# Two 5x5 convolution layers on one core: rows stored by place in the tile, and GpSimd's differences held behind VectorE's transform

## The chip, the core and the metric

The kernel runs on one core of a Trainium2 chip. The core has five engines that this kernel uses side by side, each with its own queue of instructions worked off in order: TensorE (PE, matrix products), VectorE (DVE) and GpSimd (POOL), which both do elementwise arithmetic, ScalarE (ACT, copies and activations) and SyncE (SP), which here only starts DMA transfers. Data lies in SBUF (128 partitions), matrix products land in PSUM. The metric is the time of one execution on the device, in microseconds; lower is better.

## What is computed

The input is 8 images of 32 channels, 252 x 252, in float32. Two layers are applied one after the other, each `x + conv5x5(group_norm(x))` with reflecting borders:

```python
x = x + _L0_conv_ref(_gn(x), L0_conv_weight)
x = x + _L1_conv_ref(_gn(x), L1_conv_weight)
```

`_gn` normalizes each image over 16 groups of two channels (mean and variance over two channels and all pixels). `_conv_ref` is written with FFTs in the reference, and is a 5 x 5 convolution from 32 to 32 channels.

## The kernel before

**Layout.** Rows and columns of an image are split by parity. The 128 partitions hold 4 quarters of 32 channels, one for each pair (column parity, row parity), so that a 5 x 5 filter becomes a 3 x 3 one on 126 x 126 points with 128 channels in and out. Along the rows the 3-tap filter is done as a minimal-filtering transform (Winograd's F(6,3)): a tile of 8 rows in gives 6 rows out by way of 8 products; along the columns the 3 taps are 3 accumulating matmuls.

**Steps.** An image is cut into 7 steps of 18 output rows (`GR`), each 3 tiles (`NT`) of 6 rows (`TR`). 8 images by 2 layers by 7 make 112 steps. They run in 16 phases of 7: layer 0 of one image alternates with layer 1 of the image before it. The first layer's output goes to a scratch image in DRAM, from which the second layer reads; the second layer's output goes to the result.

**What one step does.**

- `prepare` (lines 135 to 145) brings 20 rows of input into `g`: by ScalarE copies from a fetched `x` for layer 0, by one DMA from the scratch image for layer 1. In `g` row r lies at place r, so tile t's rows 0 to 5 stand together, and each row's 128 columns are contiguous.
- `differences` (336 to 346) on GpSimd: `a` (line 344) and, later, `e` (346), each one operation over 4 rows of all 3 tiles, 128 x 1536 elements, both operands in SBUF.
- `transform` (348 to 370) on VectorE: `e` again, two `v` from `e` (360, 361), `p` from `a` and two `v` from `p`, `q` from `a` and two `v` from `q`. All their operands lie in SBUF. The stt operations appear in the profile as line 358.
- `ends` (372 to 375) on GpSimd: the first and last `v` (called `v07`) from `e`.
- `conv` (378 to 435): 8 products, each of 3 matmuls (which the profile records as 6), into 8 PSUM buffers (`m`). VectorE combines them: `s1`, `d1`, sums and differences of `m3` with `m4` and `m5` with `m6` (these read one PSUM operand and one that ScalarE copied to SBUF as `a1`, `a3`, `a5`), 6 operations that write `yo[0]` to `yo[5]`, 6 that add to them, and two for `m0` and `m7`: 20 operations. `yo[j]` is row j of all three tiles; the stt ones appear as line 403.
- `to_scratch` or `to_output` sends `y` away, `output_sums` and `input_sums` gather the statistics on ScalarE.

**Order.** The kernel writes the order of each engine's queue out by hand. In step i (the loop over `steps`) VectorE does `transform` of step i + 1 and then `conv` of step i; GpSimd does `a` of step i + 2, `ends` of step i + 1, `e` of step i + 2. `a` and `e` have one buffer each, so GpSimd's next `a` waits until VectorE has read the old one, which is at `q`. In the last step of a phase VectorE also computes the next phase's normalization (`variance`, `scales`, lines 288 to 312, on 128 x 1 tiles) and adds the identity to the matrices (`add_own`, 321 to 324), and ScalarE scales the matrices (`scale_matrices`, 319). All DMAs are started from SyncE's queue, in order. They take eight semaphores in turn, and each DMA waits for the one eight before it.

Statistics of an image's input come in 8 chunks (`input_chunk`, `input_sums`), one per step from step s0 - 10 of the phase that starts at step s0, each loaded one step ahead into one of 3 buffers.

## Time and profile before

| | |
|---|---|
| time, median of 3 runs | 2537.83 us (2537.74 to 2537.83) |
| time of the profiled execution | 2537.77 us |
| its span in the profile | 2536.0 us |
| busy: PE, DVE, ACT, POOL | 1946.3, 2402.5, 1303.9, 1081.4 us |
| granted clock of TensorE, mean | 0.885 of full speed |
| DMA | 371.63 MB, mean 147 GB/s |

How to read the profile's lines. A group of instructions is "line engine operation out<-in, partitions x elements, xcount | busy us, mean ns of one | idle time of the engine before them, and what ended it". A line of the timeline is "start us, duration us, engine, line, operation, out<-in, xcount", and several equal instructions in a row are merged into one line, whose duration then reaches from the first start to the last end. A line of the waits is "who <- for whom: us in total, times, longest". A line of the windows is "from:to, length, busy us and count of PE, PEld (weight loads), DVE, ACT and POOL, the clock granted to TensorE, mean busy share of the DMA engines, GB/s". A line of the DMA issues is "out<-in, queue, xcount, KB each, median us from issue to landing". The names leave buffer numbers out: `v` is any of the v tiles.

### The profile page before, as it was taken

How to read it: one execution, taken by the hardware profiler on the slowest of the kernel's cores; microseconds unless marked ns; L12 is line 12 of the kernel's file. 1: busy time of each engine (PE TensorE's matmuls, PEld its weight loads, DVE VectorE, ACT ScalarE, POOL GpSimd, SP SyncE). 2: the span in 40 equal slices, each digit the busy share in tenths (PEclk: the TensorE clock that was granted, in tenths of full speed). 3: DMA queues.
4: the chain of work that ended last, by engine and by line, in shares of the span. 5: the costliest groups of instructions: out<-in, count | busy, mean ns of one | idle time of the engine just before them, and what ended most of it. 6: DMA issues, size and time to landing. Idle time of an engine off the chain costs nothing.

```text
span 2536.0 us, 18838 instructions
## 1 busy us (share of the span) xinstructions
PE 1946.3 (77%) x5440; PEld 1096.3 (43%) x5440; DVE 2402.5 (95%) x3473; ACT 1303.9 (51%) x1537; POOL 1081.4 (43%) x410
## 2 busy tenths in 40 slices
PE   2787868887698786888868687786877878787786
PEld 1344434444354443544434344443544444444443
DVE  6799999999999999999999999999999999999997
ACT  5885436565355644656445564455635655243233
POOL 4744444434344443443444444344444434434441
PEclk9898888889798897988979898897988889889898
DMA  7884546755466554756546476465665645344433
GB/s 224 209 207 102 131 141 197 178 102 136 155 197 141 118 171 122 201 117 131 174 153 168 103 153 192 122 172 114 129 190 168 158 108 124 106 122 143 113 97 74
DMA packets 177272, 371.63 MB, mean 147 GB/s; under 512 B 12944, under 2 KB 152464, under 8 KB 160656
## 3 DMA queue, kind: packets, MB, share of 16 engines
q1 hardware_dynamic: 177168, 370.43, 56.3%
q8 instruction: 43, 0.70, 0.1%
q14 instruction: 61, 0.50, 0.1%
HBM read 235.09 MB, written 135.28 MB: 146 GB/s over the span
## 4 chain that ended last, share of the span: by engine, by line
DVE 66%; PE 13%; issue 8%; DMA 6%; ACT 5%; SPq 1%; DVEq 0%; ACTq 0%
DVE y L403 19%; DVE v L358 16%; PE m L390 13%; DVE e L358 5%; DVE p L358 3%; DVE q L358 3%; DMA scratch<-y 3%; DVE d L411 2%; DVE mr L310 2%; DVE y L432 2%; DVE s L410 2%; DVE v L360 2%; DVE m L427 2%; DMA sx<-in_x_dram 2%; DVE v L361 2%
## 5 line engine op out<-in xcount | busy, mean ns | idle before, releaser
L390 PE MATMUL m<-v,u 128*128 128x378 f32 x5376 | 1935.0, 521 | 406.7 <-DVE d L411 288.7
L390 PEld LDWEIGHTS m<-v,u 128*128 128x128 f32 x5376 | 1082.1, 205 | 1243.5 <-DVE d L411 328.5
L344 POOL TENSOR_TENSOR a<-g 128x1536 f32<-128x1536 f32 x111 | 418.7, 3772 | 1392.4 <-DVE q L358 1303.0
L358 DVE SCALAR_TENSOR_TENSOR v<-q 128x384 f32<-128x384 f32 x224 | 469.3, 2136 | 3.9
L403 DVE SCALAR_TENSOR_TENSOR y<-m,y 128x378 f32<-128x378 f32 x672 | 370.5, 551 | 23.1
L346 POOL TENSOR_TENSOR e<-g 128x1536 f32<-128x1536 f32 x111 | 382.7, 3448 | 8.6
L468 ACT COPY o<-y 64x1134 f32<-64x1134 f32 x224 | 278.0, 1241 | 175.6 <-DVE y L434 159.3
L144 ACT COPY g<-x 64x2520 f32<-64x2520 f32 x112 | 280.4, 2503 | 14.0 <-DMA x<-in_x_dram 12.0
L414 ACT COPY a<-m 128x378 f32<-128x378 f32 x112 | 53.2, 475 | 365.7 <-PE m L390 365.1
L375 POOL TENSOR_TENSOR v<-e 128x768 f32<-128x768 f32 x111 | 236.4, 2130 | 7.7 <-DVE e L358 7.7
L275 ACT ACTIVATE junk<-y 128x2268 bf16<-128x2268 f32 x112 | 234.7, 2095 | 1.4
L358 DVE SCALAR_TENSOR_TENSOR e<-g,e 128x1536 f32<-128x1536 f32 x112 | 195.9, 1749 | 9.6 <-POOL e L346 9.6
L403 DVE SCALAR_TENSOR_TENSOR y<-m,s 128x378 f32<-128x378 f32 x336 | 185.3, 551 | 12.0
L403 DVE SCALAR_TENSOR_TENSOR y<-m,d 128x378 f32<-128x378 f32 x336 | 185.3, 551 | 11.6
L319 ACT ACTIVATE u<-u,mr 128x3072 f32<-128x3072 f32 x15 | 42.8, 2855 | 168.5 <-DVE mr L310 168.5
L269 ACT ACTIVATE sx<-sx 128x2016 f32<-128x2016 f32 x64 | 118.8, 1857 | 19.4 <-DVE sums L266 17.1
L406 ACT ACTIVATE a<-m,off 128x378 f32<-128x378 f32 x112 | 63.8, 570 | 109.6 <-PE m L390 109.4
L358 DVE SCALAR_TENSOR_TENSOR v<-p 128x384 f32<-128x384 f32 x224 | 115.2, 555 | 3.9
L296 ACT ACTIVATE std<-var 128x1 f32<-128x1 f32 x16 | 3.2, 203 | 220.9 <-DVE var L294 220.9
L358 DVE SCALAR_TENSOR_TENSOR p<-a 128x768 f32<-128x768 f32 x112 | 107.0, 955 | 0.0
L358 DVE SCALAR_TENSOR_TENSOR q<-a 128x768 f32<-128x768 f32 x112 | 106.4, 950 | 0.0
L268 ACT ACTIVATE sx<-sx 128x2016 f32<-128x2016 f32 (+1 forms) x56 | 103.6, 1850 | 3.8 <-DMA sx<-in_x_dram 3.2
(68 smaller groups left out, 1017.6 us busy)
## 6 DMA issues: line engine op xcount, KB each, us to landing
g<-scratch SPq DMA_DIRECT2D x56, 1280.0 KB, 9.7
scratch<-y SPq DMA_DIRECT2D x224, 288.0 KB, 3.9
out_dram<-o SPq DMA_DIRECT2D x224, 283.5 KB, 4.0
sx<-in_x_dram SPq DMA_DIRECT2D x56, 1008.0 KB, 7.8
x<-in_x_dram SPq DMA_DIRECT2D x88, 630.0 KB, 8.7
u<-raw SPq DMA_DIRECT2D x15, 1536.0 KB, 10.5
x<-in_x_dram SPq DMA_DIRECT2D x16, 598.5 KB, 7.0
sx<-in_x_dram SPq DMA_DIRECT2D x8, 882.0 KB, 9.8
```

The lines of the kernel that those rows point to most:

```text
L144: nc.scalar.copy(g[halves[pc], :, 1 - pc : 1 - pc + NB], t[:, :, 1 - pc : W : 2])
L268: nc.scalar.activation(t, t, AF.Identity, accum_out=st[:, 0, c : c + 1])
L269: nc.scalar.activation(t, t, AF.Square, accum_out=st[:, 1, c : c + 1])
L275: nc.scalar.activation(junk, view, (AF.Identity, AF.Square)[k], accum_out=st[:, k, T : T + 1])
L344: v.tensor_sub(rows(a), rows(high[:, :, 1:5]), rows(low[:, :, 1:5]))
L346: return lambda: v.tensor_add(rows(e), rows(high[:, :, 2:6]), rows(low[:, :, 0:4]))
L358: stt = lambda o, i0, c, i1: v.scalar_tensor_tensor(o, i0, c, i1, ALU.mult, ALU.add)
L375: v.tensor_sub(rows(vt[b, l, T].pop()), rows(e[:, :, 2:4]), rows(e[:, :, 0:2]))
L390: nc.tensor.matmul(ps, u[:, f, b3, :], vs[f][:, :, 2 - b3 : 2 - b3 + NB], start=(b3 == 0), stop=(b3 == 2),)
L403: stt = lambda o, i0, c, i1: v.scalar_tensor_tensor(o, i0, c, i1, ALU.mult, ALU.add)
L406: nc.scalar.activation(a1, m1, AF.Identity, bias=offset[b, l])
L468: nc.scalar.copy(o[halves[s], :, 1 - pc : W : 2], yr[halves[pc], s * half : (s + 1) * half, 1 : 1 + NB])
```

## The change

Rows are reordered everywhere from (tile, place in the tile) to (place in the tile, tile): in `g` (which now holds 8 places by 3 tiles, so that the two rows shared by neighbouring tiles are stored twice), `a`, `e`, `p`, `q`, `v07`, `y` and the scratch image. A slice by place, such as `yo[j]` or `a[:, 0:2]`, is now one contiguous range. In `transform` the operations are reordered, in `conv` the order of the places. `g` is filled by four ScalarE copies instead of two, or by three DMAs instead of one; the scratch image takes four DMAs per column parity and step instead of two, the result twelve per step instead of four. The input statistics' chunks come two per step, from step s0 - 7 on. And GpSimd's `a` gets an added dependency on the last operation of the last `transform`.

```diff
 GR = TR * NT
 IR = GR + 2
+DR = TR + 2
...
-        g = gpool.tile([P, IR, PB], F32, tag="g", name=f"g_{b}_{l}_{T}")
+        g = gpool.tile([P, DR, NT, PB], F32, tag="g", name=f"g_{b}_{l}_{T}")
         gt[b, l, T] = g
         if l:
-            nc.sync.dma_start(g, scratch[b][:, GR * T : GR * T + IR, :])
+            nc.sync.dma_start(g[:, 0:TR], scratch[b][:, T])
+            nc.sync.dma_start(g[:, TR:DR, 0 : NT - 1], scratch[b][:, T, 0:2, 1:NT])
+            nc.sync.dma_start(g[:, TR:DR, NT - 1], scratch[b][:, T + 1, 0:2, 0])
             return
...
-            nc.scalar.copy(g[halves[pc], :, 1 - pc : 1 - pc + NB], t[:, :, 1 - pc : W : 2])
-        pad_columns(g.rearrange("p r k -> p (r k)"), 0)
+            cols = slice(1 - pc, W, 2)
+            to = g[halves[pc], :, :, 1 - pc : 1 - pc + NB]
+            nc.scalar.copy(to[:, 0:TR], t[:, 0:GR, cols].rearrange("p (t j) w -> p j t w", j=TR))
+            nc.scalar.copy(to[:, TR:DR], t[:, 2:IR, cols].rearrange("p (t j) w -> p j t w", j=TR)[:, TR - 2 : TR])
+        pad_columns(g.rearrange("p j t k -> p (j t k)"), 0)
...
-        a = apool.tile([P, NT, 4, PB], F32, tag="a", name=f"a_{n}")
-        e = apool.tile([P, NT, 4, PB], F32, tag="e", name=f"e_{n}")
-        v.tensor_sub(rows(a), rows(high[:, :, 1:5]), rows(low[:, :, 1:5]))
+        a = apool.tile([P, 4, NT, PB], F32, tag="a", name=f"a_{n}")
+        e = apool.tile([P, 4, NT, PB], F32, tag="e", name=f"e_{n}")
+        ins = v.tensor_sub(rows(a), rows(g[:, 3:7]), rows(g[:, 1:5]))
         at[b, l, T] = a, e
-        return lambda: v.tensor_add(rows(e), rows(high[:, :, 2:6]), rows(low[:, :, 0:4]))
+        return ins, lambda: v.tensor_add(rows(e), rows(g[:, 4:8]), rows(g[:, 0:4]))
...
-        stt(rows(e), rows(low[:, :, 2:6]), -17 / 4, rows(e))
-        v.tensor_add(vs[0], e[:, :, 2], e[:, :, 1])
-        v.tensor_sub(vs[1], e[:, :, 2], e[:, :, 1])
+        stt(rows(e), rows(g[:, 2:6]), -17 / 4, rows(e))
+        stt(rows(p), rows(a[:, 0:2]), -1 / 4, rows(a[:, 2:4]))
+        v.tensor_add(vs[0], e[:, 2], e[:, 1])
+        v.tensor_sub(vs[1], e[:, 2], e[:, 1])
         yield
-        stt(rows(p), rows(a[:, :, 0:2]), -1 / 4, rows(a[:, :, 2:4]))
-        stt(vs[2], p[:, :, 0], 2.0, p[:, :, 1])
-        stt(vs[3], p[:, :, 0], -2.0, p[:, :, 1])
-        stt(rows(q), rows(a[:, :, 0:2]), -4.0, rows(a[:, :, 2:4]))
-        stt(vs[4], q[:, :, 0], 0.5, q[:, :, 1])
-        stt(vs[5], q[:, :, 0], -0.5, q[:, :, 1])
+        stt(rows(q), rows(a[:, 0:2]), -4.0, rows(a[:, 2:4]))
+        stt(vs[2], p[:, 0], 2.0, p[:, 1])
+        stt(vs[3], p[:, 0], -2.0, p[:, 1])
+        stt(vs[4], q[:, 0], 0.5, q[:, 1])
+        last["transform"] = stt(vs[5], q[:, 0], -0.5, q[:, 1])
...
-        yr = y[:, 0 : GR * PB].rearrange("p (t r k) -> p t r k", r=TR, k=PB)
-        yo = [yr[:, :, j, 1 : 1 + NB] for j in range(TR)]
+        yr = y[:, 0 : GR * PB].rearrange("p (j t k) -> p j t k", j=TR, k=PB)
+        yo = [yr[:, j, :, 1 : 1 + NB] for j in range(TR)]
...
-        for j, c in enumerate((1.0, 2.0, 4.0, 8.0, 16.0, 32.0)):
-            stt(yo[j], m3 if j % 2 else m4, c, d1 if j % 2 else s1)
+        for j in (1, 0, 3, 2, 5, 4):
+            stt(yo[j], m3 if j % 2 else m4, 2.0**j, d1 if j % 2 else s1)
...
-        for j, c in enumerate((1.0, 1 / 2, 1 / 4, 1 / 8, 1 / 16, 1 / 32)):
-            stt(yo[j], m5 if j % 2 else m6, c, yo[j])
+        for j in (5, 0, 1, 2, 3, 4):
+            stt(yo[j], m5 if j % 2 else m6, 0.5**j, yo[j])
...
-            scratch[b] = dram.tile([P, PB, PB], F32, tag="scratch", name=f"scratch_{b}")
+            scratch[b] = dram.tile([P, NG + 1, TR, NT, PB], F32, tag="scratch", name=f"scratch_{b}")
...
-                put(0, GR, J)
...
+            put(1, (T,), slice(None), slice(None))
+            put(0, (T, slice(1, TR)), slice(0, TR - 1), slice(None))
+            put(0, (T, 0, slice(1, NT)), TR - 1, slice(0, NT - 1))
+            put(0, (T + 1, 0, 0), TR - 1, NT - 1)
...
-            nc.sync.dma_start(dst[1 - pr, :, first : first + half, :], o[quads[2 * s + pr]])
+            for t in range(NT):
+                nc.sync.dma_start(dst[1 - pr, :, t, js, :], o[quads[2 * s + pr], t])
...
-                at_step = s0 - 10 + c if k > 1 else c * 5 // 8
+                at_step = s0 - 7 + c // 2 if k > 1 else c * 5 // 8
...
+    beside = mybir.DependencyInfo(mybir.DependencyClass.Sync, mybir.DependencyReason.DATA)
...
-            rest = differences(nc.gpsimd, *steps[i + 2])
+            ins, rest = differences(nc.gpsimd, *steps[i + 2])
+            tc.add_manual_dep(ins.ins, last["transform"].ins.name, beside, reason="one reader of two operands at a time")
```

The order of VectorE's queue in one transform (step 3 of image 1's first layer), with the semaphores that an instruction waits for in brackets; `v1` to `v6` are the six outputs. Before:

```order
L358 SCALAR_TENSOR_TENSOR e_1_0_3_1263<-g_1_0_3_1167,e_1_0_3_1263 128x1536 [waits Pool_49]
L360 TENSOR_TENSOR v1_1_0_3_1356<-e_1_0_3_1263 128x384 [waits DVE_49]
L361 TENSOR_TENSOR v2_1_0_3_1357<-e_1_0_3_1263 128x384
L358 SCALAR_TENSOR_TENSOR p_1_0_3_1363<-a_1_0_3_1262 128x768
L358 SCALAR_TENSOR_TENSOR v3_1_0_3_1358<-p_1_0_3_1363 128x384 [waits DVE_49]
L358 SCALAR_TENSOR_TENSOR v4_1_0_3_1359<-p_1_0_3_1363 128x384
L358 SCALAR_TENSOR_TENSOR q_1_0_3_1364<-a_1_0_3_1262 128x768
L358 SCALAR_TENSOR_TENSOR v5_1_0_3_1360<-q_1_0_3_1364 128x384 [waits DVE_49]
L358 SCALAR_TENSOR_TENSOR v6_1_0_3_1361<-q_1_0_3_1364 128x384
```

and now:

```order
L364 SCALAR_TENSOR_TENSOR e_1_0_3_1313<-g_1_0_3_1211,e_1_0_3_1313 128x1536 [waits Pool_49]
L364 SCALAR_TENSOR_TENSOR p_1_0_3_1419<-a_1_0_3_1312 128x768
L367 TENSOR_TENSOR v1_1_0_3_1412<-e_1_0_3_1313 128x384 [waits DVE_49]
L368 TENSOR_TENSOR v2_1_0_3_1413<-e_1_0_3_1313 128x384
L364 SCALAR_TENSOR_TENSOR q_1_0_3_1420<-a_1_0_3_1312 128x768
L364 SCALAR_TENSOR_TENSOR v3_1_0_3_1414<-p_1_0_3_1419 128x384 [waits DVE_49]
L364 SCALAR_TENSOR_TENSOR v4_1_0_3_1415<-p_1_0_3_1419 128x384
L364 SCALAR_TENSOR_TENSOR v5_1_0_3_1416<-q_1_0_3_1420 128x384 [waits DVE_49]
L364 SCALAR_TENSOR_TENSOR v6_1_0_3_1417<-q_1_0_3_1420 128x384
```

`p` has moved ahead of the two `v` that read `e`, and `q` ahead of the four `v` that read `p` and `q`; VectorE's waits for itself (`DVE_49`) stand at the same kind of places, with another operation between.

The end of a convolution on the same queue, just ahead of those rows, from the second half of the `y` operations to the two last products. Before:

```order
L427 TENSOR_TENSOR m5_1_0_1_1321<-a5_1_0_1_1325,m6_1_0_1_1329 128x378 [waits PE_49,Activation_49]
L428 TENSOR_TENSOR m6_1_0_1_1329<-m6_1_0_1_1329,a5_1_0_1_1325 128x378
L403 SCALAR_TENSOR_TENSOR y_1_0_1_1267<-m6_1_0_1_1329,y_1_0_1_1267 128x3x126 [waits DVE_49]
L403 SCALAR_TENSOR_TENSOR y_1_0_1_1267<-m5_1_0_1_1321,y_1_0_1_1267 128x3x126 [waits DVE_49]
L403 SCALAR_TENSOR_TENSOR y_1_0_1_1267<-m6_1_0_1_1329,y_1_0_1_1267 128x3x126 [waits DVE_49]
L403 SCALAR_TENSOR_TENSOR y_1_0_1_1267<-m5_1_0_1_1321,y_1_0_1_1267 128x3x126 [waits DVE_49]
L403 SCALAR_TENSOR_TENSOR y_1_0_1_1267<-m6_1_0_1_1329,y_1_0_1_1267 128x3x126 [waits DVE_49]
L403 SCALAR_TENSOR_TENSOR y_1_0_1_1267<-m5_1_0_1_1321,y_1_0_1_1267 128x3x126 [waits DVE_49]
L432 TENSOR_TENSOR y_1_0_1_1267<-m0_1_0_1_1341,y_1_0_1_1267 128x3x126 [waits DVE_49,PE_49]
L434 TENSOR_TENSOR y_1_0_1_1267<-m7_1_0_1_1346,y_1_0_1_1267 128x3x126 [waits DVE_49,PE_49]
```

and now:

```order
L433 TENSOR_TENSOR m5_1_0_1_1377<-a5_1_0_1_1381,m6_1_0_1_1385 128x378 [waits PE_49,Activation_49]
L434 TENSOR_TENSOR m6_1_0_1_1385<-m6_1_0_1_1385,a5_1_0_1_1381 128x378
L409 SCALAR_TENSOR_TENSOR y_1_0_1_1317<-m5_1_0_1_1377,y_1_0_1_1317 128x3x126 [waits DVE_49]
L409 SCALAR_TENSOR_TENSOR y_1_0_1_1317<-m6_1_0_1_1385,y_1_0_1_1317 128x3x126 [waits DVE_49]
L409 SCALAR_TENSOR_TENSOR y_1_0_1_1317<-m5_1_0_1_1377,y_1_0_1_1317 128x3x126
L409 SCALAR_TENSOR_TENSOR y_1_0_1_1317<-m6_1_0_1_1385,y_1_0_1_1317 128x3x126
L409 SCALAR_TENSOR_TENSOR y_1_0_1_1317<-m5_1_0_1_1377,y_1_0_1_1317 128x3x126
L409 SCALAR_TENSOR_TENSOR y_1_0_1_1317<-m6_1_0_1_1385,y_1_0_1_1317 128x3x126
L438 TENSOR_TENSOR y_1_0_1_1317<-m0_1_0_1_1397,y_1_0_1_1317 128x3x126 [waits DVE_49,PE_49]
L440 TENSOR_TENSOR y_1_0_1_1317<-m7_1_0_1_1402,y_1_0_1_1317 128x3x126 [waits PE_49]
```

The sequence of places j differs, and four of the six `y` operations and the last one no longer wait for VectorE itself.

SyncE's queue in a step of the second layer that also loads input chunks (`sx`), up to the next step's `x`. Before:

```order
L260 DMA sx_6_3585<-in_x_dram 128x2016
L140 DMA g_1_5_3617<-scratch_1294 128x2560
L471 DMA out_dram<-o_1_3633 32x9x252 x4
L118 DMA x<-in_x_dram 32x19x252
L122 DMA x<-in_x_dram 32x252
L118 DMA x<-in_x_dram 32x20x252
```

and now:

```order
L268 DMA sx_6_3797<-in_x_dram 128x2016
L268 DMA sx_7_3799<-in_x_dram 128x1764
L143 DMA g_1_5_3831<-scratch_1346 128x2304
L144 DMA g_1_5_3831<-scratch_1346 128x2x256
L145 DMA g_1_5_3831<-scratch_1346 128x2x128
L486 DMA out_dram<-o_1_3849 32x3x252 x12
```

A step now loads two chunks instead of one, fills `g` with three DMAs instead of one and sends the result with twelve instead of four.

More of the change, by code (lines that the diff above doesn't have):

```diff
@@ L333, in tile_conv_preact_x2 @@
     at, vt = {}, {}
-    rows = lambda a: a.rearrange("p t r k -> p t (r k)")
+    rows = lambda a: a.rearrange("p j t k -> p (j t k)")
+    last = {}
     def differences(v, b: int, l: int, T: int):
@@ L465, in to_output @@
         o = ot[b, T] if s == 0 else ot.pop((b, T))
-        dst = out[b].rearrange("ch (i r) w -> r ch i w", r=2)
+        o = o.rearrange("p (t j) w -> p t j w", j=TR // 2)
+        js = slice(s * TR // 2, (s + 1) * TR // 2)
+        dst = out[b].rearrange("ch (i r) w -> r ch i w", r=2)[:, :, GR * T : GR * (T + 1), :]
+        dst = dst.rearrange("r ch (t j) w -> r ch t j w", j=TR)
         for pc in range(2):
-            nc.scalar.copy(o[halves[s], :, 1 - pc : W : 2], yr[halves[pc], s * half : (s + 1) * half, 1 : 1 + NB])
+            nc.scalar.copy(
+                o[halves[s], :, :, 1 - pc : W : 2].rearrange("p t j w -> p j t w"), yr[halves[pc], js, :, 1 : 1 + NB]
+            )
         for pr in range(2):
-            first = GR * T + s * half
-            nc.sync.dma_start(dst[1 - pr, :, first : first + half, :], o[quads[2 * s + pr]])
+            for t in range(NT):
+                nc.sync.dma_start(dst[1 - pr, :, t, js, :], o[quads[2 * s + pr], t])
     phases = [(0, 0)]
@@ L531, in tile_conv_preact_x2 @@
     load_taps(1, w1, taps_at[:, 1])
-    differences(nc.vector, *steps[0])()
+    differences(nc.vector, *steps[0])[1]()
     first = transform(*steps[0])
@@ L544, in tile_conv_preact_x2 @@
     prepare(*steps[1])
-    differences(nc.gpsimd, *steps[1])()
+    differences(nc.gpsimd, *steps[1])[1]()
     fetch(*steps[3])
```

36 lines of the change are left out of this document (16 added, 20 removed).

## The prediction

> **What bounds the kernel now.** I read the page first (busy shares, costliest groups), then the list of waits, then the timeline of an ordinary step, and last the places where steps differ.
>
> ```profile
> PE 1946.3 (77%) x5440; PEld 1096.3 (43%) x5440; DVE 2402.5 (95%) x3473; ACT 1303.9 (51%) x1537; POOL 1081.4 (43%) x410
> ...
> L358 DVE SCALAR_TENSOR_TENSOR v<-q 128x384 f32<-128x384 f32 x224 | 469.3, 2136 | 3.9
> ...
> L468 ACT COPY o<-y 64x1134 f32<-64x1134 f32 x224 | 278.0, 1241 | 175.6 <-DVE y L434 159.3
> ...
> L358 DVE SCALAR_TENSOR_TENSOR e<-g,e 128x1536 f32<-128x1536 f32 x112 | 195.9, 1749 | 9.6 <-POOL e L346 9.6
> ...
> L319 ACT ACTIVATE u<-u,mr 128x3072 f32<-128x3072 f32 x15 | 42.8, 2855 | 168.5 <-DVE mr L310 168.5
> L269 ACT ACTIVATE sx<-sx 128x2016 f32<-128x2016 f32 x64 | 118.8, 1857 | 19.4 <-DVE sums L266 17.1
> ```
>
> VectorE is busy 95% and waits for almost nobody (its `e` waited for GpSimd's once, 9.6 us); TensorE waits for VectorE instead, 288.7 us in 77 places:
>
> ```profile
> PE m L390 <- DVE d L411: 288.7, 77, 6.6
> ```
>
> So a step costs what VectorE's queue costs. Its timeline, from one `e` to the next (start, duration):
>
> ```profile
> 1199.83 1.75 DVE L358 SCALAR_TENSOR_TENSOR e<-g,e 128x1536 f32<-128x1536 f32 x1
> ...
> 1201.61 0.56 DVE L360 TENSOR_TENSOR v<-e 128x384 f32<-128x384 f32 x1
> ...
> 1202.55 0.95 DVE L358 SCALAR_TENSOR_TENSOR p<-a 128x768 f32<-128x768 f32 x1
> ...
> 1203.54 1.03 DVE L358 SCALAR_TENSOR_TENSOR v<-p 128x384 f32<-128x384 f32 x2
> 1204.48 0.95 DVE L358 SCALAR_TENSOR_TENSOR q<-a 128x768 f32<-128x768 f32 x1
> ...
> 1205.47 4.28 DVE L358 SCALAR_TENSOR_TENSOR v<-q 128x384 f32<-128x384 f32 x2
> 1205.58 3.76 POOL L344 TENSOR_TENSOR a<-g 128x1536 f32<-128x1536 f32 x1 [11.55 <-DVE q L358]
> ...
> 1209.30 2.13 POOL L375 TENSOR_TENSOR v<-e 128x768 f32<-128x768 f32 x1
> 1209.68 0.54 DVE L410 TENSOR_TENSOR s<-m,a 128x378 f32<-128x378 f32 x1
> 1210.14 0.53 DVE L411 TENSOR_TENSOR d<-a,m 128x378 f32<-128x378 f32 x1
> ...
> 1211.05 0.55 DVE L419 TENSOR_TENSOR m<-m,a 128x378 f32<-128x378 f32 x1
> 1211.51 3.45 POOL L346 TENSOR_TENSOR e<-g 128x1536 f32<-128x1536 f32 x1
> ...
> 1211.63 0.55 DVE L403 SCALAR_TENSOR_TENSOR y<-m,s 128x378 f32<-128x378 f32 x1
> ...
> 1212.22 0.55 DVE L403 SCALAR_TENSOR_TENSOR y<-m,d 128x378 f32<-128x378 f32 x1
> ...
> 1220.31 0.55 DVE L434 TENSOR_TENSOR y<-m,y 128x378 f32<-128x378 f32 x1
> 1220.78 1.75 DVE L358 SCALAR_TENSOR_TENSOR e<-g,e 128x1536 f32<-128x1536 f32 x1
> ```
>
> Two things are to be seen. The pair `v<-q` takes 4.28 us where the same pair from `p` takes 1.03; it starts as GpSimd's `a` starts and ends as `a` ends. And VectorE's operations follow each other at two distances: `s` to `d` is 0.46 us, less than the operation's own 0.54, while one `y` to the next is 0.59 and `p` to its reader 0.99, slightly more than the operation. The short distance is that of operations that do not wait for the one in front. The step is 20.95 us.
>
> **The change, part by part.** How long the disputed operations take alone is shown at the kernel's start, where the two engines did not meet:
>
> ```profile
> 54.92 1.02 DVE L358 SCALAR_TENSOR_TENSOR v<-q 128x384 f32<-128x384 f32 x2
> ...
> 92.12 3.47 POOL L344 TENSOR_TENSOR a<-g 128x1536 f32<-128x1536 f32 x1
> 95.54 1.82 POOL L375 TENSOR_TENSOR v<-e 128x768 f32<-128x768 f32 x1
> 97.44 3.44 POOL L346 TENSOR_TENSOR e<-g 128x1536 f32<-128x1536 f32 x1
> ```
>
> 1. *GpSimd's wait.* `a` starts behind VectorE's last transform operation, so `v<-q` costs 1.02 instead of 4.28: **3.26 us** a step. Behind GpSimd's waiting `a` stand `ends` and `e` on its queue, and VectorE's next `e` waits for the last. The cover is the convolution's 20 operations, which read one operand from PSUM and show 0.55 us beside GpSimd's `e` (1211.63) as elsewhere. Alone the three take 97.44 + 3.44 - 92.12 = 8.76 us, plus 0.15 from release to start (1204.48 + 0.95 to 1205.58): 8.9 us behind the last transform operation. The convolution will take 20 x 0.46 = 9.2. The cover holds by 0.3 us; with the contended 3.76 and 2.13 (in which the old collision sits) the wait would show by 0.35 us. I take nothing and keep 0.35 for the range.
>
> 2. *The transform's order.* `e`, `p` and `q` are each followed by an operation that does not read them. Each distance falls by 0.12 us (1.78 to 1.66 for `e`, 0.99 to about 0.87 for `p` and `q`): **0.37 us**.
>
> 3. *The y operations.* In the program's rows each of the 12, and the two at the end, waited for the VectorE operation before it; now only the first two of each six, and one at the end, carry such a wait, and what they wait for is finished. From `m` (1211.05) to the last `y` (1220.31) there are 16 distances in 9.26 us; at 0.46 they make 7.36: **1.90 us**. The bounds are 0 (the distance belongs to the operation and its strided output) and 1.90; `s` to `d` is the nearest row with a PSUM and an SBUF operand and no wait, so I take 1.90.
>
> The ordinary step becomes 20.95 - 3.26 - 0.37 - 1.90 = **15.42 us**. To row 3 speaks a rule of the Trainium skill, page "VectorE: DVE Perf Modes", section "The DRAIN you can't avoid": a Vector operation cannot start before the pipe behind its predecessor is empty, and dropping semaphores between operations saves nothing. By it row 3 is worth 0 and the step 17.3 us. The trace disagrees for operations without a wait: `s` and `d` overlap by 0.08 us.
>
> *What is late next.* TensorE needs 48 matmuls a step:
>
> ```profile
> 1411.80 10.35 PEld L390 LDWEIGHTS m<-v,u 128*128 128x128 f32 x33 [0.17 <-issue]
> ```
>
> In an unbroken stretch 33 weight loads, one per matmul, take 10.35 us; without the last one's 0.2 us that is 32 distances of 0.317. A step is then 48 x 0.317 = 15.2 us: just below VectorE, so VectorE stays the bound and TensorE hardly idles. No lasting pitch below 15.2 is possible.
>
> *ScalarE* gets two more copies per first-layer step, smaller than the 1134-element copies of 1.24 us, so at most 2.5 us on top of 11.76:
>
> ```profile
> 1199.77:1220.72 20.95, 17.46 (x51) 10.15 (x50) 20.23 (x30) 11.76 (x15) 9.30 (x3) 0.92 0.39 106
> ...
> 120.00:140.00 20.00, 17.65 (x56) 10.15 (x55) 19.31 (x29) 18.11 (x24) 9.32 (x3) 1.00 1.04 281
> ```
>
> 14.3 of 15.4 us: hidden. In a second-layer step with two chunks of input sums (two passes of 1.86 each, and their reads, about 4.1 a chunk) beside four output copies and three of PSUM it is 8.2 + 5.0 + 1.5 = 14.7: hidden, barely.
>
> *DMAs.* The program's count on SyncE's queue goes from about 800 to 1600, with the same bytes.
>
> ```profile
> g<-scratch SPq DMA_DIRECT2D x56, 1280.0 KB, 9.7
> ...
> out_dram<-o SPq DMA_DIRECT2D x224, 283.5 KB, 4.0
> sx<-in_x_dram SPq DMA_DIRECT2D x56, 1008.0 KB, 7.8
> ```
>
> A second-layer step with two chunk loads moves 1280 + 4 x 283.5 + 2 x 1008 KB = 4.54 MB. At the 281 GB/s of the fullest stretch above that is 16.1 us, 0.7 over the step. There are 4 such steps before each of 6 images: **+17 us**. Loads run a step or more ahead, so the bounds are 0 and the stretched case below.
>
> *The scaling steps.* Once per phase, 15 times (`u<-u,mr`), VectorE computes the scales between transform and convolution, beside GpSimd:
>
> ```profile
> 1284.17 1.76 DVE L358 SCALAR_TENSOR_TENSOR e<-g,e 128x1536 f32<-128x1536 f32 x1
> ...
> 1296.16 3.08 DVE L310 TENSOR_TENSOR mr<-inv,fix 128x1 f32<-128x1 f32 x1
> ...
> 1304.72 1.40 DVE L324 TENSOR_TENSOR u<-u,own 64x512 f32<-64x512 f32 x2
> ...
> 1311.91 1.75 DVE L358 SCALAR_TENSOR_TENSOR e<-g,e 128x1536 f32<-128x1536 f32 x1
> ```
>
> Such a step takes 27.74 us. Its tiny operations read two SBUF operands and are held by GpSimd (3.08 us for one column). Now all of GpSimd's 8.9 us lie before them: 15.42 + 9.1 + 1.4 = 25.9, a saving of 1.8 only. The wait is moved, not removed.
>
> *The sum.* From the third step's `e` to the last:
>
> ```profile
> 100.91 1.76 DVE L358 SCALAR_TENSOR_TENSOR e<-g,e 128x1536 f32<-128x1536 f32 x1 [9.61 <-POOL e L346]
> ...
> 2494.83 1.75 DVE L358 SCALAR_TENSOR_TENSOR e<-g,e 128x1536 f32<-128x1536 f32 x1
> ```
>
> these are 109 of the 111 distances between 112 `e`: 15 scaling ones and 94 others. 94 x 5.53 = 520, 15 x 1.8 = 27, and two convolutions behind the last `e`, 4: 551 us less, 17 more. The profiled execution took 2537.77 us (span 2536.0), and the median is 2537.83. 2537.8 - 551 + 17 = **2004 us**.
>
> **Rivals.**
> - *The queue of DMAs stretches the heavy steps.* Each DMA waits for the eighth before it, in order. A heavy step has 12 output pieces, 3 pieces of `g` and 2 chunks: 12 x 4.0 + 3 x 9.7 + 2 x 7.8 = 92.7 us of landings, over eight 11.6 us. If they begin only when ScalarE has freed a chunk buffer, some 10 us into the step, it takes 21.6, 6.2 over: 24 steps make 149, so 1987 + 149 = 2136 us. For it: share 1.04 at 281 GB/s. Against: loads run ahead, and small pieces land faster.
> - *The y distance does not shrink* (the page's rule above): + 1.90 x 109 + 4 = 2215 us at 17.3 a step. Against: `s` and `d`.
> - *TensorE's granted clock stays below 1* (0.92 in the ordinary step above, 1.00 in the other stretch): 15.2 / 0.92 = 16.5 a step, + 1.1 x 109 = 2124 us. Against: the 33 loads show that it runs at 0.317 once it works without a gap, and the gaps go.
> - *The wait does not hold `a` back* (it names an earlier VectorE operation): 3.26 x 109 stay, 2359 us.
> - *Slower than before:* the DMA queue of the first rival becomes the bound of every step. It decides from a mean step of 20.95 + 1.5 us, which for 17 DMAs over eight slots is a mean landing of 10.6 us; the rows give 92.7 / 17 = 5.5. Price at 11 us: 17 x 11 / 8 = 23.4 a step, about 2640 us.
>
> **How the numbers follow.** Forecast 62% (from 1965, at TensorE's pitch of 15.2 and without the DMA term: 2004 - 17 - 0.2 x 109, to 2060, with GpSimd's 0.35 us on every step and half as much of small waits); stretched queue or slower TensorE 24%, up to 2150; y distance unchanged 7%; wait without effect 4%; slower 2%; some other small result 1%. The range 1965 to 2150 leaves out about 2 in 10. A measurement of this kernel tells 0.2% from no change: faster by more 0.97, within 0.01, slower 0.02.
>
> **What would show it.** `v<-q` at 0.5 us each; GpSimd's `a` released by a `v`; `y` to `y` at 0.46; `e` to `e` at 15.4, 25.9 in scaling steps; TensorE's granted clock near 1; `mr` still held for some 3 us. VectorE waiting for GpSimd's `e` breaks part 1's cover, for matmuls the claim on TensorE; steps of 18 us and more around the chunk loads would be the DMA rival. I am wrong in the main if ordinary steps stay above 17 us.

## The result, and the profile after

The changed kernel takes **2007.77 us** (median of 4 runs, 2006.09 to 2010.49) beside 2537.83 us for the kernel before on the same chip: a ratio of 0.791, 95% interval [0.790, 0.793]. The forecast was 2004. The profiled execution has a span of 2008.7 us (before 2536.0) and a mean granted TensorE clock of 0.956 (before 0.885).

First the page's busy shares and costliest groups of the changed kernel. Line 364 is what was line 358, 351 what was 344, 409 what was 403.

```profile
PE 1793.3 (89%) x5440; PEld 1045.9 (52%) x5440; DVE 1905.8 (95%) x3473; ACT 1373.6 (68%) x1649; POOL 1017.9 (51%) x410
...
L351 POOL TENSOR_TENSOR a<-g 128x1536 f32<-128x1536 f32 x111 | 384.2, 3461 | 941.9 <-DVE v L364 626.2
...
L409 DVE SCALAR_TENSOR_TENSOR y<-m,y 128x378 f32<-128x378 f32 x672 | 317.2, 539 | 0.5
...
L364 DVE SCALAR_TENSOR_TENSOR e<-g,e 128x1536 f32<-128x1536 f32 x112 | 195.8, 1748 | 14.1 <-POOL e L353 13.9
...
L364 DVE SCALAR_TENSOR_TENSOR v<-q 128x384 f32<-128x384 f32 x224 | 114.9, 553 | 0.0
```

`v<-q` has fallen from 2136 to 553 ns, GpSimd's `a` is released by a `v`, and VectorE's `e` waits for GpSimd hardly more than before (13.9 us in all, 11.5 of them once at the start). VectorE's share is still 95%: it remains what a step costs, with less to do.

The timeline of an ordinary step, with the window row of the same step (PE, PEld, DVE, ACT, POOL busy, granted clock, DMA share, GB/s):

```profile
1188.84 1.75 DVE L364 SCALAR_TENSOR_TENSOR e<-g,e 128x1536 f32<-128x1536 f32 x1
...
1194.12 1.02 DVE L364 SCALAR_TENSOR_TENSOR v<-q 128x384 f32<-128x384 f32 x2
...
1195.28 3.47 POOL L351 TENSOR_TENSOR a<-g 128x1536 f32<-128x1536 f32 x1 [6.59 <-DVE v L364]
...
1196.43 0.55 DVE L425 TENSOR_TENSOR m<-m,a 128x378 f32<-128x378 f32 x1
1196.89 0.54 DVE L409 SCALAR_TENSOR_TENSOR y<-m,d 128x378 f32<-128x378 f32 x1
1197.35 0.54 DVE L409 SCALAR_TENSOR_TENSOR y<-m,s 128x378 f32<-128x378 f32 x1
...
1200.62 3.45 POOL L353 TENSOR_TENSOR e<-g 128x1536 f32<-128x1536 f32 x1
...
1203.76 0.54 DVE L440 TENSOR_TENSOR y<-m,y 128x378 f32<-128x378 f32 x1
1204.22 1.75 DVE L364 SCALAR_TENSOR_TENSOR e<-g,e 128x1536 f32<-128x1536 f32 x1
```

```profile
1188.84:1204.22 15.38, 15.38 (x50) 9.16 (x49) 15.38 (x30) 13.29 (x18) 8.71 (x3) 1.00 0.87 172
```

The step is 15.38 us (before 20.95). One `y` follows another at 0.46 us. TensorE runs unbroken at a granted clock of 1.00. GpSimd's `e` ends at 1200.62 + 3.45 = 1204.07, and VectorE's next `e` starts 0.15 later, which is also 0.46 after the last `y`. So VectorE's and GpSimd's chains end within 0.2 us of each other, and TensorE, at 48 matmuls of 0.317 us, needs 15.2 us for the same step: three engines now have almost the same length.

*The scaling steps* are of two kinds. Timeline of one that enters a second layer, 25.94 us from `e` to `e`, and of one that enters a first layer, 22.50:

```profile
1031.65 3.43 POOL L351 TENSOR_TENSOR a<-g 128x1536 f32<-128x1536 f32 x1 [7.12 <-DVE inv L314]
1031.68 3.42 DVE L315 TENSOR_TENSOR fix<-inv 128x1 f32<-128x1 f32 x1
1035.04 1.81 POOL L381 TENSOR_TENSOR v<-e 128x768 f32<-128x768 f32 x1
1035.13 1.73 DVE L316 TENSOR_TENSOR fix<-fix,var 128x1 f32<-128x1 f32 x1
...
1036.92 3.42 POOL L353 TENSOR_TENSOR e<-g 128x1536 f32<-128x1536 f32 x1
1037.08 3.27 DVE L318 TENSOR_TENSOR mr<-inv,fix 128x1 f32<-128x1 f32 x1
```

```profile
916.28 0.16 DVE L315 TENSOR_TENSOR fix<-inv 128x1 f32<-128x1 f32 x1
916.32 3.43 POOL L351 TENSOR_TENSOR a<-g 128x1536 f32<-128x1536 f32 x1 [7.11 <-DVE inv L314]
916.48 3.29 DVE L316 TENSOR_TENSOR fix<-fix,var 128x1 f32<-128x1 f32 x1
919.70 1.81 POOL L381 TENSOR_TENSOR v<-e 128x768 f32<-128x768 f32 x1
...
919.99 1.54 DVE L318 TENSOR_TENSOR mr<-inv,fix 128x1 f32<-128x1 f32 x1
```

Three operations of one column each have two SBUF operands. In the first kind each of them is held by one of GpSimd's three operations. In the second the first `fix` starts 0.04 us ahead of GpSimd's `a` and costs 0.16 instead of 3.42, and the next two are held by `a` and by `ends`. The three take 4.99 us together instead of 8.42: the whole difference of the two kinds. They are 8 and 7 of the 15 steps.

*The long steps.* Of the 94 other steps 20 take over 16.2 us, 49.4 us more in all than at 15.38: three right behind the start (8.7 us, ScalarE late with the second image's chunks), and two or three in each of six cycles of two phases (one in a seventh). Two of the latter, a second-layer step of 18.03 and a later one of 18.30:

```profile
1067.64 0.56 ACT L412 ACTIVATE a<-m,off 128x378 f32<-128x378 f32 x1
1068.25 18.05 PE L396 MATMUL m<-v,u 128*128 128x378 f32 x56 [1.33 <-ACT a L412]
...
1074.75 2.50 ACT L481 COPY o<-y 64x1134 f32<-64x1134 f32 x2
...
1077.28 0.55 DVE L409 SCALAR_TENSOR_TENSOR y<-m,d 128x378 f32<-128x378 f32 x1 [2.55 <-ACT o L481]
```

```profile
1098.41 11.72 SPq L486 DMA_DIRECT2D out_dram<-o  x12
...
1110.18 0.43 SPq L121 DMA_DIRECT2D x<-in_x_dram  x1
...
1119.29 2.30 ACT L151 COPY g<-x 64x2268 f32<-64x2268 f32 x1 [3.63 <-DMA x<-in_x_dram]
...
1126.73 0.56 DVE L424 TENSOR_TENSOR m<-a,m 128x378 f32<-128x378 f32 x1 [2.73 <-ACT a L420]
```

In the first, ScalarE comes from a chunk's sums to `a1` late, then to the output copies, and VectorE waits 2.55 us for the `y` buffer that those copies read. In the second, the twelve output DMAs take 11.72 us of SyncE's queue, the `x` behind them is issued late, and the wait passes from ScalarE's copy into `g` by way of its `a3` to VectorE. The queue's own waits in that stretch (1098 to 1110.2) say why:

```profile
SPq L486 <- DMA g<-scratch: 4.3, 2, 3.9
SPq L486 <- DMA sx<-in_x_dram: 1.7, 1, 1.7
```

For 6.0 us the output pieces wait until the DMAs eight places ahead of them, a chunk and two pieces of `g`, have landed. Without such waits twelve pieces take 5.6 us of the queue (5.62 at 1126.84 in experiment 5). So it is not their number alone that makes `x` late.

### The profile page after: what moved, and what is told of

Same layout as the page of the kernel before. It is cut to its first block, busy times and chain, and to the rows that moved or that the text cites. A ratio compares the mean times of both kernels' runs of the same rounds, so it can differ in the third digit from the quotient of the medians.

```text
span 2008.7 us, 19828 instructions
## 1 busy us (share of the span) xinstructions
PE 1793.3 (89%) x5440; PEld 1045.9 (52%) x5440; DVE 1905.8 (95%) x3473; ACT 1373.6 (68%) x1649; POOL 1017.9 (51%) x410
## 2 busy tenths in 40 slices
DMA packets 225664, 386.43 MB, mean 192 GB/s; under 512 B 25488, under 2 KB 200848, under 8 KB 212624
## 4 chain that ended last, share of the span: by engine, by line
DVE 39%; PE 33%; DMA 10%; ACT 9%; issue 4%; POOL 2%; SPq 2%; DVEq 0%; ACTq 0%; POOLq 0%
PE m L396 33%; DVE y L409 13%; DMA g<-scratch 7%; DVE v L364 4%; DVE e L364 3%; DVE mr L318 2%; DVE fix L316 2%; ACT g L151 2%; DMA x<-in_x_dram 2%; DVE p L364 2%; DVE q L364 2%; DVE m L424 1%; DVE fix L315 1%; DVE m L425 1%; ACT sx L276 1%
## 5 line engine op out<-in xcount | busy, mean ns | idle before, releaser
L396 PE MATMUL m<-v,u 128*128 128x378 f32 x5376 | 1785.0, 493 | 97.8 <-ACT u L327 32.3
L396 PEld LDWEIGHTS m<-v,u 128*128 128x128 f32 x5376 | 1034.2, 194 | 832.0 <-DVE u L332 34.8
L351 POOL TENSOR_TENSOR a<-g 128x1536 f32<-128x1536 f32 x111 | 384.2, 3461 | 941.9 <-DVE v L364 626.2
L409 DVE SCALAR_TENSOR_TENSOR y<-m,y 128x378 f32<-128x378 f32 x672 | 317.2, 539 | 0.5
L151 ACT COPY g<-x 64x2268 f32<-64x2268 f32 x112 | 257.7, 2301 | 41.3 <-DMA x<-in_x_dram 33.8
L364 DVE SCALAR_TENSOR_TENSOR e<-g,e 128x1536 f32<-128x1536 f32 x112 | 195.8, 1748 | 14.1 <-POOL e L353 13.9
L381 POOL TENSOR_TENSOR v<-e 128x768 f32<-128x768 f32 x111 | 207.0, 1865 | 2.1 <-DVE e L364 2.1
L409 DVE SCALAR_TENSOR_TENSOR y<-m,s 128x378 f32<-128x378 f32 x336 | 181.2, 539 | 0.0
L277 ACT ACTIVATE sx<-sx 128x2016 f32<-128x2016 f32 x64 | 118.9, 1858 | 19.5 <-DVE sums L274 17.2
L364 DVE SCALAR_TENSOR_TENSOR v<-q 128x384 f32<-128x384 f32 x224 | 114.9, 553 | 0.0
L152 ACT COPY g<-x 64x756 f32<-64x756 f32 x112 | 100.0, 893 | 0.0
```

The costliest lines, as they stand in the source:

```text
L151: nc.scalar.copy(to[:, 0:TR], t[:, 0:GR, cols].rearrange("p (t j) w -> p j t w", j=TR))
L152: nc.scalar.copy(to[:, TR:DR], t[:, 2:IR, cols].rearrange("p (t j) w -> p j t w", j=TR)[:, TR - 2 : TR])
L277: nc.scalar.activation(t, t, AF.Square, accum_out=st[:, 1, c : c + 1])
L351: ins = v.tensor_sub(rows(a), rows(g[:, 3:7]), rows(g[:, 1:5]))
L364: stt = lambda o, i0, c, i1: v.scalar_tensor_tensor(o, i0, c, i1, ALU.mult, ALU.add)
L381: v.tensor_sub(rows(vt[b, l, T].pop()), rows(e[:, 2:4]), rows(e[:, 0:2]))
```

## Experiments

Each ran beside the kernel before. "Step" is the distance from `e` to `e` in an ordinary step of the trace. Edits are to the changed kernel unless said otherwise, and shown without their side lines; "..." marks what is left out. The changed kernel itself, run again between them, took 2007.29 us (2005.60 to 2009.64):

> The changed kernel once more, on the chip of the three runs beside it: 2008 us, ordinary step 15.38, steps near the chunk loads 16.5 to 18.8.

**1. Without the wait** (`e1_no_wait`).

```diff
-            tc.add_manual_dep(ins.ins, last["transform"].ins.name, beside, reason=...)
```

> The changed kernel without GpSimd's added wait; everything else stays. My account: GpSimd's a is released at q again, two operations of VectorE earlier than in the kernel before, and VectorE's v operations behind it are held for a's 3.46 us: v<-p or v<-q means rise from 0.55 to over 2 us, an ordinary step goes from 15.4 to 18.7 us or, if ends holds them a second time, 20.5; in all 2370 to 2560 us. Rival (the layout, not the wait, ended the collision): 2008 us and v at 0.55.

2349.89 us (2 runs), ratio 0.926 [0.922, 0.929]. The rival falls: the wait is needed, and is worth 342 us in the changed kernel. My range for it was missed by 20 us. Two steps of the same trace, with the same instructions in the same order:

```profile
227.10 4.28 DVE L364 SCALAR_TENSOR_TENSOR v<-p 128x384 f32<-128x384 f32 x2
227.33 3.64 POOL L351 TENSOR_TENSOR a<-g 128x1536 f32<-128x1536 f32 x1 [15.44 <-DVE q L364]
230.92 2.15 POOL L381 TENSOR_TENSOR v<-e 128x768 f32<-128x768 f32 x1
231.31 5.88 DVE L364 SCALAR_TENSOR_TENSOR v<-q 128x384 f32<-128x384 f32 x2
233.15 3.63 POOL L353 TENSOR_TENSOR e<-g 128x1536 f32<-128x1536 f32 x1
```

```profile
560.88 1.02 DVE L364 SCALAR_TENSOR_TENSOR v<-p 128x384 f32<-128x384 f32 x2
561.11 5.05 POOL L351 TENSOR_TENSOR a<-g 128x1536 f32<-128x1536 f32 x1 [4.99 <-DVE q L364]
561.82 1.02 DVE L364 SCALAR_TENSOR_TENSOR v<-q 128x384 f32<-128x384 f32 x2
```

In the first VectorE is held three times, by `a`, by `ends` and by `e`: three of its four `v` take 3.81, 2.18 and 3.78 us instead of 0.55, which makes 15.38 + 8.1 = 23.5 us for the step. I had expected one or two of these holds in every step; there were three of them, but only in 44 of the 94 steps that don't scale. In the second GpSimd's `a` is held, until VectorE's four `v` are nearly done, VectorE loses nothing, and the step takes 15.38.

**2. The wait alone** (`e2_wait_only`), the added wait put into the kernel before, with its old layout and orders:

```diff
+            tc.add_manual_dep(ins.ins, last["transform"].ins.name, beside, reason=...)
```

> The kernel before with GpSimd's wait alone. My account: v<-q falls from 2136 to about 553 ns, the ordinary step from 20.95 to 17.7 us (y operations still 0.59 apart), scaling steps stay near 28; about 2237 us, 2214 if every second scaling step is shorter. Rival (the collision only moves to other operations of VectorE): no change, 2538 us.

2223.95 us, ratio 0.876 [0.875, 0.878]; step 17.70, `v<-q` 558 ns. As expected: the step loses 3.25 us where the forecast said 3.26. Its scaling steps, too, are of two kinds, 28.12 and 24.68.

**3. Waits between the y operations** (`e3_y_waits`): in each six, every `y` operation after the first waits for the one in front.

```diff
-            stt(yo[j], m3 if j % 2 else m4, 2.0**j, d1 if j % 2 else s1)
+            front = behind(stt(yo[j], m3 if j % 2 else m4, 2.0**j, d1 if j % 2 else s1), front)
...
-            stt(yo[j], m5 if j % 2 else m6, 0.5**j, yo[j])
+            front = behind(stt(yo[j], m5 if j % 2 else m6, 0.5**j, yo[j]), front)
```

> The changed kernel, in which each of the six y operations again waits for the one in front of it; same layout, same order. My account (the wait for the operation in front costs the distance): ten distances a step grow from 0.46 to 0.585, the step by 1.25 us, in all about 2146 us. Rival (the page's rule that semaphores between operations cost nothing; the contiguous output made the distance short): 0.46 stays, 2008 us.

2110.84 us, ratio 0.832 [0.830, 0.833]; step 16.66. A group of such operations in its timeline:

```profile
239.33 0.54 DVE L414 SCALAR_TENSOR_TENSOR y<-m,d 128x378 f32<-128x378 f32 x1
239.91 0.55 DVE L414 SCALAR_TENSOR_TENSOR y<-m,s 128x378 f32<-128x378 f32 x1
240.50 0.55 DVE L414 SCALAR_TENSOR_TENSOR y<-m,d 128x378 f32<-128x378 f32 x1
```

The distance is 0.58 instead of 0.46, with the same operands and the same duration: ten waits cost 1.28 us, 0.13 each. Term 3's cause is shown, and the rival falls. The total rose by 103 instead of 139, since a slower step covers most of the long ones: the 94 other steps lie 17 us in all above their ordinary length, in the changed kernel 58.

**4. The orders undone** (`e4_orders_undone`), `transform` and the places j in the old order, layout and wait kept:

```diff
-        for j in (1, 0, 3, 2, 5, 4):
+        for j in range(TR):
...
-        for j in (5, 0, 1, 2, 3, 4):
+        for j in range(TR):
...
-        stt(rows(p), rows(a[:, 0:2]), -1 / 4, rows(a[:, 2:4]))
         v.tensor_add(vs[0], e[:, 2], e[:, 1])
         v.tensor_sub(vs[1], e[:, 2], e[:, 1])
         yield
-        stt(rows(q), rows(a[:, 0:2]), -4.0, rows(a[:, 2:4]))
+        stt(rows(p), rows(a[:, 0:2]), -1 / 4, rows(a[:, 2:4]))
         stt(vs[2], p[:, 0], 2.0, p[:, 1])
         stt(vs[3], p[:, 0], -2.0, p[:, 1])
+        stt(rows(q), rows(a[:, 0:2]), -4.0, rows(a[:, 2:4]))
```

> The changed kernel with the order of the transform and of the places j as before; layout and wait stay. My account: five distances a step again have a reader right behind its writer (e, p, q, and the first y of each six), 0.12 us each, 0.6 a step: about 2073 us. Rival (the order matters through when TensorE's buffers come free or GpSimd starts): no such sum; a change beyond 100 us or none.

2052.92 us, ratio 0.808 [0.807, 0.810]; step 16.03, 0.65 longer (0.6 expected; the total rose by 45 instead of 65, as in 3). So of the 2.32 us between the wait alone (17.70) and the whole change (15.38), the orders bring 0.65 and the layout the other 1.67: contiguous places are what freed most `y` operations of their waits. In this run's trace 4 of the 14 `y` operations of a step still wait for VectorE itself, in experiment 2 all 14. The new orders in the old layout were not run.

**5. The old chunk schedule** (`e5_chunks_as_before`), one chunk per step from s0 - 10 on:

```diff
-                at_step = s0 - 7 + c // 2 if k > 1 else c * 5 // 8
+                at_step = s0 - 10 + c if k > 1 else c * 5 // 8
```

> The changed kernel with the input statistics' chunks scheduled as before: one a step from step s0 - 10, so that two fall beside ScalarE's copies of x. Account A (two chunks in one step make ScalarE late, and TensorE and VectorE wait for it): the long steps at s0 - 6 vanish (3 us in each of 6 cycles, and most of the 38 us that steps around the loads are over 15.4), while step s0 - 3 gets 17 us of ScalarE and loses about 2: 1980 to 1995 us. Account B (SyncE's queue, with twelve output pieces in each second-layer step, brings x late whatever the chunks do): the long steps at s0 - 3 stay, and only some 18 us go: about 1990 with step s0 - 3 still at 18. Rival (the schedule does not matter): 2008 us.

2009.73 us, ratio 0.792 [0.791, 0.793]: the rival's number, though not its reason. The long steps were not removed but moved, to the two behind a scaling step into a second layer, in six cycles (17.4 to 18.7, and 19.0). Two chunks a step was not by itself the cost. Those of the second kind, at s0 - 3 (17.7 to 18.6), are back at 15.46 in all six cycles, with the result's twelve pieces unchanged, so the pieces alone do not make them.

**6. Scales ahead of GpSimd** (`e7_scales_first`): in a scaling step GpSimd's `a` waits for the last scale instead of the last `v`.

```diff
+        for p in late.get(i, []):
+            scales(*p)
         if i + 2 < N:
             ins, rest = differences(nc.gpsimd, *steps[i + 2])
...
             rest()
-        for p in late.get(i, []):
-            scales(*p)
...
-        v.scalar_tensor_tensor(mr[:, 1:2], ...)
+        last["transform"] = v.scalar_tensor_tensor(mr[:, 1:2], ...)
```

> The changed kernel with VectorE's scale computation ahead of GpSimd's a in the scaling steps (a waits for its last operation there). My account: the tiny operations take 0.15 us each, the scaling step falls from 25.9 and 22.5 to about 18.2 us, 15 of them: 92 us less, 1916 us. Rival (GpSimd's e, now later, or TensorE's late matrices end the step instead): steps above 21 us, 1960 us or more.

1970.20 us, ratio 0.776 [0.775, 0.777]: a gain of 37 of the 92 expected, in the rival's range. The tiny operations take 0.16 us each now, but scaling steps still take 21.8. Its timeline shows who is held next:

```profile
549.43 1.81 POOL L381 TENSOR_TENSOR v<-e 128x768 f32<-128x768 f32 x1
...
550.42 5.21 DVE L332 TENSOR_TENSOR u<-u,own 64x512 f32<-64x512 f32 x2
...
551.32 3.77 POOL L353 TENSOR_TENSOR e<-g 128x1536 f32<-128x1536 f32 x1
```

GpSimd, now later, meets `add_own`, which also reads two SBUF operands: 5.21 us for the pair where it was 1.39 before the shift. A wait was moved once more.

**7. Both of these, chunks spread** (`e8_both`): as 6, with chunks at s0 - 10 + c * 7 // 8.

> Scales first as in the run before, and the chunks spread over steps s0 - 10 to s0 - 4, two in the first of them alone, where ScalarE has neither copies of x nor output copies. Account A: all steps around the loads fall to 15.4, another 35 us less: about 1880 us. Account B: step s0 - 3 stays long, about 1898 us.

1948.23 us, ratio 0.768 [0.767, 0.769]. All long steps but one in a cycle (18.0, at s0 - 6, not at the s0 - 3 of account B) and those at the start are gone; scaling steps are 21.85 as in 6, which is why the total lies above what was expected.

**8. add_own ahead as well** (`e9_own_first`): as 7, and in a scaling step GpSimd's `e` waits for the second `add_own`.

```diff
-            nc.vector.tensor_add(u[h, :, 1 + pc, h], u[h, :, 1 + pc, h], own[h])
+            last["own"] = nc.vector.tensor_add(u[h, :, 1 + pc, h], u[h, :, 1 + pc, h], own[h])
...
-        if i + 2 < N:
+        if i + 2 < N and i not in late:
             rest()
...
+        if i + 2 < N and i in late:
+            tc.add_manual_dep(rest().ins, last["own"].ins.name, beside, reason=...)
```

> The kernel e8_both (1948.2 us), and in each of the 15 scaling steps GpSimd's e waits for VectorE's second add_own, as a waits for the last scale. In e8 and e7 the pair of add_own takes 5.2 us there, from 550.42 to 555.63 in e7's trace, the first released when GpSimd's ends is over and the second when its e is over. Theory (what the scaling steps still cost is one more operation with two SBUF operands held by GpSimd): the pair at about 1.4 us, scaling steps of 15.4 + 6 x 0.19 + 2 x 0.6 = 17.7 instead of 21.85, the total 1948 - 15 x 4.1 = 1886. Rival (TensorE has to wait for the new matrices anyway, 2.5 us per phase, and its pitch of 15.2 leaves it 0.2 us a step to catch up): the pair is short but the scaling step or the two behind it lose up to 2.5 us again, 1886 to 1924.

1919.13 us, ratio 0.756 [0.755, 0.757], in the rival's range, but only in part for its reason: the list of waits has TensorE waiting 23.0 us in all for the matrices, and 27.3 us for the offset's copy (4.6 in experiment 7). Scaling steps fell to 18.7 (the pair 2.08, its first half still held by `ends`), 47 us less in all, but the two steps behind those into a second layer rose to 17.2 to 17.9 and 19.0, 17.7 us back.

**9. No chunk behind the scaling step** (`e10_chunks_spread`): as 8, with chunks in s0 - 12 to s0 - 8 and s0 - 5 to s0 - 3.

> The kernel e9_own_first, and the eight chunks of input sums in steps s0-12 to s0-8 and s0-5 to s0-3, none in the two steps behind a scaling step into a second layer. In e8 one step per cycle remained long, 18.0 us: VectorE's first y waited 2.5 us for the output copy that ScalarE made 2.5 us late, behind the last output sums of the first layer and a chunk. Theory (ScalarE's queue in those two steps is what makes the long steps): no step above 16 us beside the scaling ones and those at the start, 6 x 2.6 = 16 us less than e9. Rival (the heavier first-layer steps, which have four copies into g, now overflow instead): long steps of 17 to 18 us move to s0-12 and s0-11, and the total stays within 5 us of e9.

1919.41 us, ratio 0.756 [0.755, 0.757]: no change, and the long steps stayed where they were. Neither account held, only the rival's total; the timeline of the stretch named the cause. The last line is the window 549 to 554, with the clock in its third figure from the end:

```profile
548.76 0.14 ACT L338 COPY off<-po 128x1 f32<-128x1 f32 x1
...
548.95 37.41 PE L396 MATMUL m<-v,u 128*128 128x378 f32 x109 [4.30 <-ACT off L338]
...
557.58 0.56 DVE L424 TENSOR_TENSOR m<-a,m 128x378 f32<-128x378 f32 x1 [1.91 <-PE m L396]
...
577.64 0.55 DVE L409 SCALAR_TENSOR_TENSOR y<-m,d 128x378 f32<-128x378 f32 x1 [3.52 <-ACT o L481]
```

```profile
549.00:554.00 5.00, 5.00 (x8) 2.79 (x9) 5.00 (x8) 0.50 (x1) 0.00 (x0) 0.50 0.47 175
```

The chunk in the scaling step itself (s0 - 8) stands on ScalarE's queue in front of the offset's copy; TensorE waits 4.3 us for it and runs unbroken afterwards, but not at full speed at first: up to 554 its granted clock is 0.50, and eight matmuls take 5.2 us from start to start instead of 2.5. So the stop costs 2.6 us more than its own length, and at 15.2 us a step TensorE makes up only 0.2 us a step. The trace of experiment 5 has the same wait (6 times, 22.2 us in its list of waits).

**10. The offset early** (`e12_offset_early`): as 9, `find_offset` in front of the second output sums, chunks in s0 - 13 to s0 - 9 and s0 - 5 to s0 - 3.

```diff
         def after_5():
+            for p in late.get(i, []):
+                find_offset(*p)
             if done:
...
-        for p in late.get(i, []):
-            find_offset(*p)
```

> The kernel e10_chunks_spread (1919.4 us), with the offset's product and its ScalarE copy in front of the second output sums instead of behind the chunk's sums, and no chunk in the scaling step into a second layer (steps s0-13 to s0-9 and s0-5 to s0-3). In e10's trace TensorE waits 4.3 us behind such a scaling step for that offset (548.76, behind two passes of output sums and two of a chunk), and is then unbroken for 37.4 us; VectorE waits for it 1.9 us in the next step and 3.5 us, by way of the output copies, in the one after. Theory (the late offset makes these long steps, since TensorE at 15.2 a step has nothing to catch up with): both steps at 15.4, 6 x (2 + 3.6) = 33 us less, 1886. Rival (ScalarE's queue itself is late there, whatever the offset does): the second of the two stays at 17 to 18 us, about 1902.

1902.73 us, ratio 0.750 [0.748, 0.751]. Both steps behind the scaling step are at 15.38: the theory held there, with the offset's copy at 539.97 and TensorE running through.

```profile
534.59 44.70 PE L396 MATMUL m<-v,u 128*128 128x378 f32 x140
...
539.97 0.16 ACT L338 COPY off<-po 128x1 f32<-128x1 f32 x1
```

Since the offset and the chunk in s0 - 8 were moved together, their shares aren't told apart. About 12 us of the expected 33 went back: five chunks in a row beside the copies into `g` make steps of 16.2 and 17.0 at their end, in five of the cycles. That the total is the rival's number (1902) is therefore an accident: the steps that it names are short. This is the fastest version that ran.

**11. The wait on an earlier v** (`e11_wait_on_p`), in the changed kernel:

```diff
-        stt(vs[2], p[:, 0], 2.0, p[:, 1])
+        last["transform"] = stt(vs[2], p[:, 0], 2.0, p[:, 1])
...
-        last["transform"] = stt(vs[5], q[:, 0], -0.5, q[:, 1])
+        stt(vs[5], q[:, 0], -0.5, q[:, 1])
```

> The changed kernel, with GpSimd's a waiting for the first v from p instead of the last from q, so that it arrives while three of VectorE's v are still to come. In the kernel without the wait half of the ordinary steps took 23.5 us (a from 3.6 us on, VectorE's v held) and half 15.38 (a recorded at 5.05 us, the v not held), with the same order and the same 0.14 us from q's end to a's start. Theory 1 (whoever has the port keeps it while its operations follow each other without a gap, so VectorE's four v, none of which waits for the one before, hold a back): every step 15.4, v from q 553 ns, a about 4.5 us, total within 3 us of 2007. Theory 2 (each meeting falls one way or the other): two kinds of steps again, v from q above 1000 ns on average, total 2100 to 2350. Theory 3 (GpSimd always gets in between two operations): v held in every step, about 20 us and more a step, above 2450.

2028.28 us, ratio 0.799 [0.798, 0.800]. The costliest groups of its page:

```profile
L351 POOL TENSOR_TENSOR a<-g 128x1536 f32<-128x1536 f32 x111 | 482.1, 4343 | 864.0 <-DVE v L364 575.3
...
L364 DVE SCALAR_TENSOR_TENSOR v<-q 128x384 f32<-128x384 f32 x224 | 115.0, 554 | 0.0
```

Theory 1 holds for the step: 15.38, and where GpSimd meets VectorE's chain it is GpSimd that is held, about 1.1 us (85 of the 111 `a` take 4.3 us or more). It missed the total by 20 us, for a reason outside the transform: all 15 scaling steps are at 25.7, none at 22.5 (385.8 us in all, 365.1 in the changed kernel).

Not tried: the result's twelve DMAs as fewer, with two chunks a step. It would tell how much of the second kind of long step is the number of pieces; experiment 5 shows only that the pieces don't make it without the second chunk.

## Why the prediction was right, and where it was not

The same stretch that the sum was made for, third `e` to last, went from 2393.9 to 1868.3 us. Summed from its distances:

| | predicted | measured |
|---|---|---|
| 94 other steps, at the ordinary step's pitch | -520 | 94 x (15.38 - 20.95) = -524 |
| their long ones | +17 | +49 |
| 15 scaling steps | -27 | 365.1 - 416.1 = -51 |
| ahead of the third `e` | 0 | +2 |
| behind the last `e` | -4 | -4 |
| sum | -534 | -528 (of the spans: -527) |

1. *GpSimd's wait, 3.26 us*: right, and shown (17.70 in experiment 2; 342 us lost without it). The cover by the convolution held, by even less than the 0.3 us said: in the step shown GpSimd's `e` ends 0.15 us before VectorE's next `e` starts. The rival in which the wait does not hold `a` back is excluded by `v<-q`.
2. *The transform's order, 0.37*: `e` to `p` is 1.66, `p` to the next 0.87, as said. With the y orders undone too, experiment 4 gives 0.65; 0.37 by itself was not run.
3. *The y operations, 1.90*: from `m` to the last `y` 1203.76 - 1196.43 = 7.33 us, predicted 7.36. The Trainium skill, page "VectorE: DVE Perf Modes", section "The DRAIN you can't avoid", says that a semaphore between operations costs nothing extra; experiment 3 measures 0.13 us for each wait on the operation in front, and the measurement decides. The same section also says that an operation that is not held starts earlier, which the prediction did not tell and with which the 0.46 us agrees. The rival of 2215 us falls.
4. *TensorE*: its pitch never bound an ordinary step, and its clock there is 1.00; the rival of 2124 us falls for the step. The clock is not near 1 everywhere, as was said: behind a stop of 4.3 us eight matmuls ran at 0.50 (experiment 9). That, and that only 0.2 us of a step of 15.4 are left to catch up, made the late offset so dear in experiments 5, 8 and 9.
5. *Scaling steps, "the wait is moved, not removed"*: the mechanism was right, and 25.94 is exact for 8 of them. The term was mis-sized for the other 7, 22.50: the forecast took it that all of GpSimd's 8.9 us lie before the tiny operations, but one slips in ahead of `a` by 0.04 us. -51 instead of -27.
6. *ScalarE, "hidden, barely"*, and *the DMA term, +17*: the step that failed. The long steps cost 49 us, and what was late is the order of a queue. I compared ScalarE's busy time with the step's length (14.7 us forecast, 14.71 in the window of the 18.03 us step) and left out that its queue is in order, so that a chunk's sums delay `a1` and the output copies, and VectorE by way of the `y` buffer. ScalarE waits for no DMA there: it is at work without a pause from 1057.80 to 1068.20, most of it on sums. So bandwidth, on which the +17 was worked out, is not what this kind ran into (287 GB/s at a share of 0.86 in the window of the step). In the other kind SyncE's queue brings `x` late, behind output pieces that wait for landings. There the DMA engines' share was 0.92 at 295 GB/s in the 11.72 us and 1.03 at 262 GB/s in the 18.30 us step, so how much of it is bandwidth stays open. Experiments 5, 7 and 10 move these steps about with the chunks' places. The bytes were not the same either, as the forecast had it: 386.43 MB instead of 371.63, since `g`'s shared rows are now read twice.
7. The stretched DMA queue (2136 us) and the slower case (2640 us) did not come; the second kind of long step is the mechanism of the first of them (a DMA waits for the eighth before it), at 17 us in all instead of 149. The price of the slower case was not summed rightly: 109 distances of 23.4 us, with the start and the end as they were, would be some 2690 us, not 2640.

Points 5 and 6 were wrong by 24 and 32 us in opposite directions, and so the total came out within 4 us. The step's parts were right; the rest of the agreement is luck.
